# A retention and FFN sandwich: the output projection by seven products of halves, and a reordered first FFN round

## The chip, the cores and the metric

The kernel runs on one core of a Trainium2 chip. The metric is the device time of one execution in microseconds (us), as the median of several runs. A profile is one further execution, taken by the hardware profiler. The engines are named as in the profile: PE is TensorE (matmuls), PEld its weight loads, DVE is VectorE, ACT is ScalarE, POOL is GpSimd, and SP is the engine whose queue issues nearly all DMA transfers.

## The reference

The input x holds 4 sequences of 1024 tokens with 512 features, all float32. Two residual branches follow each other: a gated retention layer and a gated FFN.

```python
def _L0_attn_ref(x, Wq, Wv, Wo, Wg, ln_gamma, ln_beta, beta):
    lam = _decay_lambda(beta)
    q = (x @ Wq.T).reshape(Bsz, Ls, NHEAD, HEAD_DIM)
    v = (x @ Wv.T).reshape(Bsz, Ls, NHEAD, HEAD_DIM)
    ret = _retention_scan(v, lam)          # state = lam * state + v, along the tokens
    out = (q * ret).reshape(Bsz, Ls, D)
    out = _layernorm(out, ln_gamma, ln_beta)
    g = jax.nn.silu(x @ Wg.T)
    out = out * g
    return out @ Wo.T

def _L0_ffn_ref(x, gate_w, up_w, down_w, gate_scale, up_scale, down_scale):
    gate = jax.nn.silu(_quantized_matmul(x, gate_w, gate_scale))   # 512 -> 1536
    up = _quantized_matmul(x, up_w, up_scale)                      # 512 -> 1536
    fuse = gate * up
    return _quantized_matmul(fuse, down_w, down_scale)             # 1536 -> 512, weights rounded to fp8

x = x + _layernorm(_L0_attn_ref(_layernorm(x), ...))
x = x + _layernorm(_L0_ffn_ref(_layernorm(x), ...))
```

## The kernel before

The 4096 tokens are cut into eight blocks of 512 (`NB`), and a block into four token tiles of 128 (`NS`). A block passes through a retention part (class `Retention`) and an FFN part (class `Ffn`). The main loop, lines 985 to 1200, runs over blocks `t` and, within one, over twelve steps `i`, one for each 128 of the 1536 hidden features. I call the twelve steps of one `t` a round. In round `t` the FFN of block `t` (`f`, fed by `a`) is computed, and between its matmuls the retention part of block `t+1` (`b`), the end of the FFN of block `t-1` (`l`), and the loads and the first norm of block `t+2` (`n`) are interleaved. The order is written out by hand: every call goes through `InOrder` (line 66), which keeps each engine's instructions in program order. So an instruction that waits holds back everything behind it on its engine, and a DMA that waits holds back the later ones of SP.

In each step TensorE does a group `pfg` (gate), a group `pfu` (up) and, two steps late, a group `pd` (down). Each is eight matmuls with 512 moving columns, for which the normalized input and the fused product are split in two parts of reduced precision: an upper part, cast by ScalarE (`upper_of`, the cast in `fuse`), and a remainder, subtracted on VectorE (`rest_of`, `rest`). The groups `pfg` and `pfu` write into the two PSUM buffers `pf`. ScalarE applies Silu to `pfg` (into a `gate` tile, tag `sg`, three buffers), and VectorE multiplies with `pfu`.

The projections q, v and g of blocks 0 and 1 are plain float32 matmuls. From block 2 on (`FAST = 2`), `product` computes them in the Winograd form of Strassen's scheme: features and tokens are halved, and seven products of halves, each of eight passes of 256 columns, take the place of eight. Sums of the weight halves are made once (`weight_sums`) and kept in DRAM (`keep_sums`); sums of the input halves are made on POOL for each block (`input_sums`, into `t_sums`). The operands are fetched through a ring of four tiles (`w_ring`): after each product the fetch for the fourth product ahead is issued on SP (`fetch_weights`). Partial results are added on ScalarE and VectorE in `mids`.

The output projection `o` (line 657) is a plain float32 group for each token tile, called in steps 7 to 10. Then, for each token tile: `o_moments` (mean and variance of the PSUM tile on VectorE, the power -1/2 on POOL), `x1_of` (norm, from block 2 on with `center_scale` on VectorE; residual addition on POOL; the store `kept` on SP), `x1_moments`, `x1n_of` (norm), and the turn to features on partitions. Tiles 0 to 2 are turned by VectorE and DMA (`move_x1n`, `turn_by_blocks`: a 32x32 transpose, four stores `mxs` to DRAM, one load), tile 3 by TensorE (`turn_x1n`, rows `pt`). `upper_of` and `rest_of` then fill `x1nT`, which the first `pfg` of the next round reads.

Meanwhile `norm_x` and `send_x` make and store the normalized tiles of `n` in steps 6 to 9; from block 3 on the tile and its transposed copy lie in a single buffer:

```python
self.pair = work.tile([P, 2, D], F32, tag="xn", name=f"xn_{self.t}_{s}", bufs=1)
```

`fetch_x` loads them back turned (`xnT`). Two more threads run in rounds 0 and 1. `rounds` and `units` round the FFN weights in pieces on VectorE and ScalarE in round 0. `find_over` reads the rounded weights on ScalarE in round 1 (24 passes, rows `seen`; the list `look` says how many in which step). The mean and the variance over features for block `b` are matmuls with a constant matrix, rows `mu` and `var`; their input is split by `halves`, called in step 3 before `mean` and in step 4 before `var`.

## Time and profile before

| quantity | value |
|---|---|
| median of 3 runs | 984.01 us (983.93 to 984.02) |
| the profiled execution | 983.95 us |
| its span, first to last instruction | 982.1 us |
| granted TensorE clock | 0.998 |
| matmuls `po` (8 passes for each of 32 token tiles) | 256 records, 114.5 us busy |
| matmuls `pt` (turns on TensorE) | 44 records, 6.8 us busy |
| products of blocks 2 to 7 | 21 for each block |
| rounds 2 to 5, one round | 117.5 us |

The page of the profile gives busy times of each engine, the chain of waits that ended last, and groups of like instructions. All kernel instructions are recorded under line 74, since `InOrder` issues them; so groups are told apart by tile names (`po<-wo_sb,y` is written to `po`, reading `wo_sb` and `y`). In a timeline, a row has the start, the duration, the engine and the operation; `x8` is a run of eight, and a bracket at its end tells how long the engine stood idle before it and who ended that wait. Matmuls are pipelined and the ends of their records are modelled, so that the distance between starts is the surer measure.

### The profile page before, as it was taken

To read this page: it belongs to the slowest core of one execution; us is meant where nothing else is said; L and a number is where in the kernel's file an instruction comes from. 1 tells how busy PE (TensorE), PEld (TensorE's weight loads), DVE (VectorE), ACT (ScalarE), POOL (GpSimd) and SP (SyncE) were. 2 spreads that over 40 slices of the span, in tenths; PEclk is the share of its full clock that TensorE was granted. 3 is DMA by queue.
4 is the path that set the end of the run, shared out by engine and by line. 5 is a ranking of instruction groups with operands and counts; after the bars stand their busy time and mean duration, and the time that the engine had idled before them with its cause. 6 is when DMAs were issued, how large, how long until landed. Compare 5 with 4: busy or idle time off the path is not lost.

```text
span 982.1 us, 11265 instructions
## 1 busy us (share of the span) xinstructions
PE 963.9 (98%) x3950; PEld 734.3 (75%) x3950; DVE 663.3 (68%) x1019; ACT 369.9 (38%) x556; POOL 266.7 (27%) x346
## 2 busy tenths in 40 slices
PE   9999999989999999999999999999999999999996
PEld 7456656678876888678876788768887788877885
DVE  5996979655667667675686666766667765756445
ACT  3546655467645125221432215321152211512223
POOL 1405121412324033240513305133141322322020
PEclk9999999999999999999999999999999999999999
DMA  9311413752416426253243623245241542213021
GB/s 300 119 65 65 130 63 94 228 161 75 151 53 156 128 82 225 80 143 120 86 129 93 176 77 116 87 131 151 83 150 59 135 140 76 75 37 113 1 86 43
DMA packets 90936, 110.07 MB, mean 112 GB/s; under 512 B 8064, under 2 KB 55424, under 8 KB 90880
## 3 DMA queue, kind: packets, MB, share of 16 engines
q1 hardware_dynamic: 90016, 108.70, 36.5%
q8 instruction: 31, 0.51, 0.2%
q10 hardware_dynamic: 864, 0.66, 0.2%
q14 instruction: 25, 0.20, 0.1%
HBM read 76.56 MB, written 32.77 MB: 111 GB/s over the span
## 4 chain that ended last, share of the span: by engine, by line
PE 84%; DVE 7%; ACT 4%; POOL 2%; DMA 1%; issue 1%; SPq 0%; DVEq 0%; POOLq 0%; ACTq 0%
PE pfu L74 15%; PE pfg L74 15%; PE pd L74 15%; PE pq L74 10%; PE pv L74 10%; PE po L74 9%; PE pg L74 9%; DVE scr L74 1%; DVE st L74 1%; DVE gate L74 1%; PE idle L74 1%; DVE xs L74 1%; DVE fuse L74 1%; DMA xnT<-mx 1%; POOL sqsum L74 1%
## 5 line engine op out<-in xcount | busy, mean ns | idle before, releaser
L74 PE MATMUL pfu<-x1nT,up_sb 128*128 128x512 f32 x768 | 211.5, 417 | 0.3 <-DVE gate L74 0.3
L74 PE MATMUL pfg<-x1nT,gate_sb 128*128 128x512 f32 x768 | 195.4, 396 | 1.4 <-ACT gate L74 1.4
L74 PE MATMUL pd<-down_sb,fuse 128*128 128x512 f32 x720 | 186.5, 400 | 0.0
L74 PEld LDWEIGHTS pfu<-x1nT,up_sb 128*128 128x128 f32 x768 | 144.4, 188 | 43.0 <-issue 13.4
L74 PEld LDWEIGHTS pfg<-x1nT,gate_sb 128*128 128x128 f32 x768 | 144.2, 188 | 31.7 <-ACT gate L74 1.8
L74 PEld LDWEIGHTS pd<-down_sb,fuse 128*128 128x128 f32 x720 | 134.9, 188 | 27.4
L74 ACT CAST fuse<-gate 128x512 fp32r<-128x512 f32 x90 | 55.7, 618 | 235.5 <-DVE gate L74 235.5
L74 ACT ACTIVATE gate<-pfg,gs_sb 128x512 f32<-128x512 f32 x96 | 65.7, 685 | 193.0 <-PE pfg L74 192.9
L74 DVE SCALAR_TENSOR_TENSOR gate<-pfu,us_sb,gate 128x512 f32<-128x512 f32 x96 | 71.7, 747 | 72.3 <-PE pfu L74 69.8
L74 PE MATMUL po<-wo_sb,y 128*128 128x512 f32 x256 | 114.5, 592 | 0.0
L74 POOL TENSOR_SCALAR mv<-mv 128x1 f32<-128x1 f32 (+1 forms) x82 | 19.9, 243 | 299.0 <-DVE mv L74 298.0
L74 PEld LDWEIGHTS po<-wo_sb,y 128*128 128x128 f32 x256 | 48.2, 189 | 50.3 <-issue 46.3
L74 DVE TENSOR_TENSOR fuse<-gate,fuse 128x512 fp32r<-128x512 f32 x90 | 74.5, 827 | 12.1 <-ACT fuse L74 12.1
L74 POOL TENSOR_TENSOR ysum<-y 128x256 f32<-128x256 f32 (+1 forms) x14 | 14.0, 1000 | 189.9 <-DVE y L74 189.9
L74 POOL TENSOR_TENSOR x<-x,x1n 128x512 f32<-128x512 f32 x32 | 46.8, 1463 | 45.6 <-DVE x1n L74 36.7
L74 DVE BATCH_NORM_STATS2 st<-x 128x6 f32<-128x512 f32 x64 | 43.6, 681 | 13.7 <-POOL x L74 11.3
L74 POOL TENSOR_TENSOR mv<-mv,nhalf 128x1 f32<-128x1 f32 (+1 forms) x75 | 46.3, 617 | 6.2
L74 PE MATMUL pg<-t_sums,w_ring 128*128 128x256 f32 x192 | 45.6, 380 | 0.6 <-ACT mids L74 0.6
L74 PE MATMUL pv<-t_sums,w_ring 128*128 128x256 f32 x192 | 45.4, 379 | 0.8 <-POOL t_sums L74 0.8
L74 PE MATMUL pq<-t_sums,w_ring 128*128 128x256 f32 x192 | 45.3, 379 | 0.0
L74 PEld LDWEIGHTS pg<-t_sums,w_ring 128*128 128x128 f32 x192 | 35.9, 189 | 7.3 <-ACT mids L74 2.0
L74 PEld LDWEIGHTS pv<-t_sums,w_ring 128*128 128x128 f32 x192 | 36.2, 189 | 6.6 <-POOL t_sums L74 1.0
(150 smaller groups left out, 1337.3 us busy)
## 6 DMA issues: line engine op xcount, KB each, us to landing
kept<-x SPq DMA_DIRECT2D x32, 256.0 KB, 2.1
x<-kept SPq DMA_DIRECT2D x32, 256.0 KB, 4.1
x<-in_x SPq DMA_DIRECT2D x28, 256.0 KB, 4.1
out<-d SPq DMA_DIRECT2D x27, 256.0 KB, 2.0
xnT<-mx SPq DMA_DIRECT2D x24, 256.0 KB, 4.9
w_ring<-dsum_v SPq DMA_DIRECT2D x24, 256.0 KB, 2.7
w_ring<-dsum_q SPq DMA_DIRECT2D x24, 256.0 KB, 2.6
w_ring<-dsum_g SPq DMA_DIRECT2D x24, 256.0 KB, 2.7
```

The source lines that it names most:

```text
L74: return lambda *args, **kwargs: tc.keep_in_program_order(op(*args, **kwargs))
```

## The change

The output projection of blocks 2 to 7 becomes a fourth family of products, "o": seven products with halves of y as stationary operand (`left`) and halves or sums of the output weights from the ring as moving operand. `output_sums` makes four weight sums in place in round 1, step 0, and `keep_sums("o")` stores them. `y_sums` makes two sums of y on VectorE (step 6) and two on POOL (step 7). `add_o` copies two products on ScalarE and adds five on VectorE; the results lie in `mids` and take the place of the PSUM tiles `po`. The products stand three in step 7, three in step 8, one in step 9. What follows is regrouped by pairs of token tiles: `x1_of` for these blocks goes to ScalarE (`shift_scale`), tile 2 is turned on TensorE as well as tile 3, and the loads of tiles 0 and 1 are issued after all eight of their stores. For `n`, the norms of tiles 1 and 2 fall in step 7, tile 3 and `fetch_x` in step 8. In step 11 the fused product comes ahead of the norm of tile 3, the remainder of step 10 comes after both, and the v products are taken in the order 1, 2, 6.

In round 0, `halves` is called at the end of steps 2 and 3, with the weight rounding of step 3 moved behind the mean and partly behind the second call; the gate tile g of chunk 0 for block 1 takes a buffer of tag `tok` instead of `sg`; in steps 10 and 11 the stores of the g sums come after the stores of tile 2's turn, the norm of tile 3 goes to VectorE, and a product stands ahead of its turn. In round 1 the passes of `find_over` are distributed otherwise.

```diff
-        sp.dma_start(dst, m)
+        return lambda: sp.dma_start(dst, m)
...
-    order = [("v", j) for j in (1, 6, 2, 7, 4, 5, 3)]
+    order = [("v", j) for j in (1, 2, 6, 7, 4, 5, 3)]
     order += [("q", j) for j in (1, 6, 2, 7, 4, 5, 3)]
     order += [("g", j) for j in (1, 2, 6, 7, 4, 5, 3)]
-    banks = {"v": {1: 0, 6: 1, 5: 0}, "q": {1: 1, 6: 0, 5: 1}, "g": {1: 0, 6: 0, 5: 1}}
+    order += [("o", j) for j in (1, 2, 6, 5, 3, 7, 4)]
+    banks = {
+        "v": {1: 0, 6: 1, 5: 0}, "q": {1: 1, 6: 0, 5: 1},
+        "g": {1: 0, 6: 0, 5: 1}, "o": {1: 0, 6: 1, 5: 0},
+    }
...
+    def output_sums():
+
+        v = woT.rearrange("(c p) f -> p c f", p=P)
+        b11, b12, b21, b22 = (wo_sb[:, i : i + 2, o : o + H] for i in (0, 2) for o in (0, H))
+        operands["o"] = {1: v[:, 0:2, 0:H], 2: v[:, 2:4, 0:H], 3: v[:, 2:4, H:D]}
+        made["o"] = {5: b11, 7: b12, 6: b22, 4: b21}
+        dve.tensor_tensor(b11, b12, b11, ALU.subtract)
+        dve.tensor_tensor(b12, b22, b12, ALU.subtract)
+        dve.tensor_tensor(b22, b22, b11, ALU.subtract)
+        dve.tensor_tensor(b21, b21, b22, ALU.subtract)
...
+                    if k == "o":
+                        left, right = self.left[j][:, c, ts(o, P)], w[:, c, :]
+                    else:
+                        left, right = w[:, c, ts(o, P)], self.right[j][:, c]
...
+            if k == "o":
+                return self.add_o(j, bank)
             c12, p1, s167 = (mids[:, m] for m in (1, 2, 3))
+            if k == "v" and self.t == FAST:
+
+                if j == 1:
+                    self.p1 = work.tile([P, 2, H], F32, tag="rstd", name="p1", bufs=1)
+                p1 = self.p1
...
+        def y_sums(self, *which):
+            y = self.y
+            a11, a12, a21, a22 = (y[:, c : c + 2, ts(h, H)] for h in range(2) for c in (0, 2))
+            s1, s2, s3, s4 = (t_sums[:, k] for k in range(4))
+            self.left = {1: a11, 2: a12, 3: s4, 4: a22, 5: s1, 6: s2, 7: s3}
+            ops = {
+                1: (dve, s1, a21, a22, ALU.add), 2: (dve, s2, s1, a11, ALU.subtract),
+                3: (pool, s3, a11, a21, ALU.subtract), 4: (pool, s4, a12, s2, ALU.subtract),
+            }
+            for k in which:
+                engine, dst, x, y, op = ops[k]
+                engine.tensor_tensor(dst, x, y, op)
...
+        def add_o(self, j, bank):
+
+            by_tile = mids.rearrange("p (r s) h f -> p r s h f", r=2)
+            c11, c12, c21, c22 = (by_tile[:, r, :, h, :] for r in range(2) for h in range(2))
+            if j == 1:
+                act.copy(c21, bank)
+            elif j == 2:
+                act.copy(c11, bank)
+            elif j == 6:
+                dve.tensor_tensor(c12, bank, c21, ALU.add)
...
+            if j in (3, 4):
+                for s in (0, 1) if j == 3 else (2, 3):
+                    self.po[s] = mids[:, s].rearrange("p h f -> p (h f)")
...
             home = big if self.t == 0 and c == 3 else work
-            tag = "fuse" if home is big else "sg"
-            self.g[c] = home.tile([P, TB], F32, tag=tag, name=f"g_{self.t}_{c}", bufs=3)
+            tag, bufs = ("fuse", 3) if home is big else ("tok", 4) if self.t == 1 and c == 0 else ("sg", 3)
+            self.g[c] = home.tile([P, TB], F32, tag=tag, name=f"g_{self.t}_{c}", bufs=bufs)
...
         def x1_of(self, s):
             self.x1n[s] = work.tile([P, D], F32, tag="tok", name=f"x1n_{self.t}_{s}", bufs=4)
-            self.center(self.x1n[s], self.po.pop(s), self.mvo[s])
+            center = shift_scale if self.fast else self.center
+            center(self.x1n[s], self.po.pop(s), self.mvo[s])
...
+        def x1n_of(self, s, center=None):
+            (center or self.center)(self.x1n[s], self.xt[s], self.mvo.pop(s))
...
+    look = [(2, 3), (2, 3), (2, 3), (1, 0), (0, 0), (0, 2)]
+    look += [(0, 1), (0, 1), (1, 0), (1, 1), (0, 0), (1, 0)]
...
-            if t > 0 and (t > 1 or i):
+            if t > 0 and (t > 1 or i) and not (fast and i == 11):
...
-                if i == 10:
-                    keep_sums("g")
...
-            if fast and i in (0, 1, 2, 3, 4, 5, 6):
+            if fast and i < 10:
                 b.product()
...
             if b and not fast and i == 3:
-                b.halves()
-                units()
-                rounds(3, now=False)
                 units()
                 b.g_of(0)
                 b.mean()
                 b.center_y()
+                n.stats(2)
                 n.stats(3)
                 n.rstd()
                 n.shift()
             if b and not fast and i == 4:
-                b.halves()
                 rounds(3, now=False)
...
-            if b and 7 <= i <= 10:
+            if b and not fast and 7 <= i <= 10:
                 b.o(i - 7)
             if b and i == 8:
                 b.new_x1nT()
-            if b and i >= 8:
+            if b and not fast and 8 <= i < 11:
                 b.x1n_of(i - 8)
-            if b and 8 <= i < 11:
-                b.move_x1n(i - 8)
-            if b and i >= 9:
+            if b and not fast and 8 <= i < 11:
+                load = b.move_x1n(i - 8)
+                if i == 10:
+                    keep_sums("g")
+                load()
+            if b and not fast and 9 <= i < 11:
                 b.upper_of(i - 9)
-            if b and 7 <= i <= 10:
+            if b and not fast and 7 <= i <= 10:
                 b.o_moments(i - 7)
-            if n and i == 11:
-                n.input_sums(1, 2, 3, 4)
+            if fast and i == 7:
+                b.y_sums(3, 4)
+            if fast and i == 9:
+                b.x1_moments(0)
+                b.x1_moments(1)
+            if fast and i == 10:
+                b.x1_of(2)
+                b.x1_of(3)
             units()
             f.up(i)
+            if n and i == 11:
+                n.input_sums()
+                n.product()
             f.fuse(i)
+            if b and i == 11:
+                b.x1n_of(3, center_scale)
+            if fast and i == 11:
+                f.rest(10)
+            if n and i == 11:
+                n.input_sums(*((3, 4) if fast else (1, 2, 3, 4)))
+            if t == 0 and i == 11:
+                b.upper_of(2)
+            if fast and i == 9:
+                loads = []
+                for s in range(2):
+                    b.x1n_of(s)
+                    loads.append(b.move_x1n(s))
+                for load in loads:
+                    load()
+                if n:
+                    n.input_sums(1, 2)
+            if fast and i == 11:
+                for s in range(2):
+                    b.upper_of(s)
+                    b.rest_of(s)
             if t == 0 and i == 4:
                 b.rstd_y()
-            if n and i == 11:
-                n.product()
-                if t:
-                    b.turn_x1n(3, "pf")
-                    b.upper_of(3)
+            if n and t and i == 11:
+                b.turn_x1n(2, "pf")
+                b.upper_of(2)
             if t == 2 and i == 0:
                 next(passing)
             if fast and i < 6:
             if fast and i == 6:
                 b.gate_y(0)
                 b.gate_y(1)
+                b.y_sums(1, 2)
+            if n and t > 0 and i == 8:
+                n.norm_x(3, True)
+                n.send_x(3)
+            if fast and i in (7, 8):
+                b.product()
+            if n and t > 0 and i == 8:
+                n.fetch_x()
+            if fast and i == 8:
+                b.o_moments(0)
+                b.o_moments(1)
+                b.x1_of(0)
+                b.x1_of(1)
+            if fast and i == 9:
+                b.o_moments(2)
+                b.o_moments(3)
+            if fast and i == 10:
+                b.x1_moments(2)
+                b.x1_moments(3)
+                b.x1n_of(2)
             if t == 0:
-                if i < 8 and i != 3:
+                if i == 3:
+                    rounds(2, now=False)
+                    b.halves()
+                    units()
+                    rounds(1, now=False)
+                elif i < 8:
                     rounds(3, now=False)
+                if i == 2:
+                    b.halves()
                 f.rest(i)
-                if i < 3:
+                if i < 2:
                     n.stats(i)
-            for _ in range((look[i] + 1) // 2 if t == 1 else 0):
-                next(search)
 
             if l and not b and i in (4, 5):
                 l.stats(2 * i - 8)
                     l.rstd()
             if n and i == 6:
                 n.new_xnT()
-            if b and 7 <= i <= 10:
+            if b and not fast and 7 <= i <= 10:
                 b.x1_of(i - 7)
-            if b and i >= 9:
+            if b and not fast and i >= 9:
                 b.rest_of(i - 9)
-            if n and t > 0 and 6 <= i <= 9:
-                n.norm_x(i - 6, True)
-                n.send_x(i - 6)
+            if n and t > 0 and i in (6, 7):
+                for s in ([0], [1, 2])[i - 6]:
+                    n.norm_x(s, True)
+                    n.send_x(s)
+            for _ in range(look[i][1] if t == 1 else 0):
+                next(search)
             if t == 0 and i in (5, 6):
                 n.send_x(2 * i - 10)
                 n.send_x(2 * i - 9)
-            if n and i == (9 if t else 7):
+            if n and t == 0 and i == 7:
                 n.fetch_x()
             if b and n and i == 11 and t:
-                b.rest_of(3)
+                b.rest_of(2)
             if t == 0 and i in (8, 9):
                 keep_sums("vq"[i - 8])
 
             elif l and i < 2 and (b or i == 0):
                 l.down(NI - 2 + i if b else NI - 1)
             if b and not n and i == 11:
+                b.turn_x1n(2)
+                b.upper_of(2)
+                b.rest_of(2)
                 b.turn_x1n(3)
                 b.upper_of(3)
                 b.rest_of(3)
                 f.down(NI - 2)
 
-            if t == 0 and i == 11:
+            if n and i == 11:
+                if t == 0:
+                    n.product()
                 b.turn_x1n(3, "pf")
                 b.upper_of(3)
                 b.rest_of(3)
-            if fast and i < 3:
+            if fast and (i < 3 or i in (7, 8)):
                 b.product()
             if fast and i == 2:
                 l.stats(2)
                 b.var()
                 b.rstd_y()
             if n and i == 11:
-                n.products(2)
+                n.products(2 if t else 1)
             if n and t > 0 and i == 5:
                 n.stats(0)
                 n.stats(1)
+            if t == 1 and i == 0:
+                output_sums()
+                keep_sums("o")
             if t == 0 and i == 9:
                 w_ring = wpool.tile([P, RING, 2, H], F32, tag="wv_sb", name="w_ring")
             if t == 0 and i in (9, 10):
```

## The prediction

> **What bounds the kernel now.** I read the page first: busy shares, then the chain of waits.
>
> ```profile
> PE 963.9 (98%) x3950; PEld 734.3 (75%) x3950; DVE 663.3 (68%) x1019; ACT 369.9 (38%) x556; POOL 266.7 (27%) x346
> PE 84%; DVE 7%; ACT 4%; POOL 2%; DMA 1%; issue 1%; SPq 0%; DVEq 0%; POOLq 0%; ACTq 0%
> ```
>
> TensorE is the bound. A busy share hides where it waits, so next the windows of one FFN round each:
>
> ```profile
> 100.00:206.00 106.00, 100.16 (x372) 68.87 (x371) 84.05 (x117) 56.45 (x86) 28.20 (x33) 1.00 0.43 133
> 322.00:440.00 118.00, 117.91 (x501) 93.31 (x500) 79.91 (x127) 36.10 (x56) 34.79 (x45) 1.00 0.44 132
> 440.00:557.00 117.00, 116.91 (x495) 92.44 (x494) 79.40 (x123) 33.76 (x52) 34.80 (x45) 1.00 0.39 114
> ```
>
> Columns: length, then PE, PEld, DVE, ACT, POOL busy. The first row (round 0, old path) lacks 6 us; later rounds lack 0.1, so there only fewer matmuls or new waits can matter. The timeline of PE at step 11 of a later round gives the prices:
>
> ```profile
> 546.08 1.98 PE L74 MATMUL pfg<-x1nT,gate_sb 128*128 128x512 f32 x8
> 547.90 1.98 PE L74 MATMUL pfu<-x1nT,up_sb 128*128 128x512 f32 x8
> 549.71 1.89 PE L74 MATMUL pv<-xnT,w_ring 128*128 128x256 f32 x8
> 551.69 0.63 PE L74 MATMUL pt<-ident,x1n 128*128 128x128 f32 x4
> 552.08 2.09 PE L74 MATMUL pd<-down_sb,fuse 128*128 128x512 f32 x8
> 554.00 1.89 PE L74 MATMUL pv<-t_sums,w_ring 128*128 128x256 f32 x8
> 555.73 1.89 PE L74 MATMUL pv<-xnT,w_ring 128*128 128x256 f32 x8
> ```
>
> Read starts, since ends overlap: a gate, up or down group costs 1.82 us, a product 1.73 (554.00 to 555.73). The same timeline has the waits of PE, all in rounds 0 and 1:
>
> ```profile
> 118.43 0.50 PE L74 MATMUL mu<-half,mean_r 128*128 128x512 f32 x1 [0.49 <-DVE half L74]
> ...
> 128.43 0.50 PE L74 MATMUL var<-half,mean_r 128*128 128x512 f32 x1 [0.58 <-ACT half L74]
> ...
> 143.60 2.14 PE L74 MATMUL pfg<-x1nT,gate_sb 128*128 128x512 f32 x8 [1.41 <-ACT gate L74]
> ...
> 196.84 0.66 PE L74 MATMUL pt<-ident,x1n 128*128 128x128 f32 x4 [0.65 <-ACT x1n L74]
> 198.25 1.99 PE L74 MATMUL pv<-t_sums,w_ring 128*128 128x256 f32 x8 [0.75 <-POOL t_sums L74]
> 201.66 1.96 PE L74 MATMUL pv<-xnT,w_ring 128*128 128x256 f32 x8 [1.42 <-ACT x1nT L74]
> ...
> 252.96 1.99 PE L74 MATMUL pg<-t_sums,w_ring 128*128 128x256 f32 x8 [0.64 <-ACT mids L74]
> ```
>
> **What the Trainium skill says.** "SBUF — State Buffer", section "Who interferes with whom": VectorE with two SBUF inputs, or in a 2-port mode, and GpSimd exclude each other for whole instructions. The trace agrees: a fuse remainder that takes 0.66 took 1.78 at 546.52, until POOL's addition ended.
>
> ```profile
> 546.09 1.67 POOL L74 TENSOR_TENSOR x<-x,x1n 128x512 f32<-128x512 f32 x1 [1.61 <-DVE x1n L74]
> 546.52 1.78 DVE L74 TENSOR_TENSOR fuse<-gate,fuse 128x512 fp32r<-128x512 f32 x1
> 550.07 1.47 DVE L74 TENSOR_SCALAR x1n<-x,mv 128x512 f32<-128x512 f32 x1 [0.95 <-POOL mv L74]
> ```
>
> "TensorE: Matmul & The Clock Gate", "Back-to-back issue gap", has the isolated gap follow the free size (N/2.4 + 2.5 ns). In the trace half the width costs half: 3.44 us for eight passes of 512, 1.73 for eight of 256, so halving the tile isn't taxed.
>
> **The change, part by part.**
>
> Output projection of blocks 2 to 7. Removed: four groups po, each 3.44 (four steps of 8.89 less three groups of 1.82): 13.76. Added: seven products of 1.73: 12.11. So -1.65 a block. Also added: token tile 2 is turned on TensorE, not by DMA. At 904.15 a turn with no wait put 0.35 before one group and 0.12 on it: +0.45. Net -1.2 a block, -7.2 in six. The DMA turn it saves costs PE nothing today.
>
> New waits of these steps. I count from the start of step 7's gate group (510.52 in round 3), other durations from rows.
> - Product 1 needs y of chunk 1. VectorE finished it at 512.75, +2.23. Its first two passes last 0.43, not the 0.86 of po's, so it asks earlier: 0.2 a block.
> - VectorE then makes two sums (0.69 each) and POOL two (1.3 to 1.45), which shut VectorE out: the step 7 gate product ends near +7.6 instead of +6.4. Behind it on ScalarE: the fuse cast, the copy of products 1+2 (0.59), then two xn (0.81 each). Blocks from 3 on hold xn and its turned copy in one single-buffered pair, so the second xn waits for the first's store: turned at +10.4, landed 2.3 later, +12.8; xn 13.6, turn 14.3, addition of product 6 15.0, remainder 15.7, addition of product 5 16.4. Product 3 accumulates in product 5's bank and stands at +16.0. Wait 0 to 0.8; I take 0.3.
> - Moments, ScalarE's x1, POOL's addition, second moments and x1n of tile 2 end near +38.5; its turn stands at +39.3. Tile 3's x1n, once shut out by POOL's input sums (1.3), ends at +40.7; turn +41.7. Then four remainders of 0.68 behind step 10's end at +45.4, one group of the next round needs them at +45.8, and product 6's addition ends +47.6 where product 7 stands at +47.5. Slack 0.4 with two exclusions counted; bounds 0 and 1.6, I take 0.4.
> Sum 0.9 a block, 5.4 in six: this part nets -1.8. In round 6 no next block's products stand between the last turn and the next gate group, only one down group of 1.82; VectorE has less there too, and I keep the same 0.9.
>
> Moved on SP, in order of issue: the stores of xn go out in steps 6 to 8 and the four loads of xnT in step 8, ahead of both kept stores; the two tiles' eight mxs stores follow the x1n of step 9 (near +29.5 and +31), their loads come after all eight, at about +33.3 and +35.6, and land 2.7 to 3.7 later, by +39.3. ScalarE wants them after the fuse cast, at +40.7: covered by 1.4; if that cover goes, the next round's first gate group waits one for one. xnT, asked for at +22, lands by +28 (5.8 at most from the trace's chain) and is wanted by POOL at +28.4 and by PE at +37.6.
>
> Cost nothing: the eight more weight loads' traffic (2.6 to 3.1 us landing against four products of ring), since fetches are issued four products ahead; POOL's two sums, behind 27% load; ScalarE's x1 passes (0.20+0.29+0.78 for each of four tiles, 5.1 a block, which frees VectorE of four of 0.80), 38% load. If the queue of SP blocked (kept waits for POOL's addition), the ring still covers over 10 us. Four sums of wo in round 1 (0.69 each) and their stores lie in VectorE's gaps; without these, up to 2.8. The search keeps its 24 passes, moved.
>
> Round 0, steps 3 to 6. mu started its group 1.03 late (117.15 to 118.77 is 1.62; 482.59 to 483.18, unhindered, 0.59); halves now stand before that step's rounding. var: 1.56 late (next group due at 127.94, came at 129.50); its halves stand before one rounding. Step 6's gate group: 1.56 (143.60 against 142.04): ScalarE's Silu waited for a buffer that g of chunk 0 held; that tile moves to the tok buffers. Bounds 0 and 4.15. VectorE is late next: reciprocal (3.35) and rounding stay, 84 of 106 us are busy. I take 3.6.
>
> Round 0, step 11: waits with pipeline loss 1.0, 0.95 and 1.7. x1n of tile 3 goes from ScalarE to VectorE, a product comes before the turn, tile 2's move is sent before the four stores of wg sums (mxs started at 191.41, after stores that began at 188.70; its landing ended the last wait). Next: POOL's second sum at about 198.2 and remainder 3. Bounds 0 and 3.65; I take 3.1. Step 11's 0.32 for DVE gate stays.
>
> Round 1: ScalarE's copy for the second product of g is freed of one search pass (1.56+0.19) ahead of it: 0.8 goes. xn is fetched a step earlier: the 0.29 at 314.61 goes, 0.4 with loss. Together 1.2.
>
> Sum: -1.8 -3.6 -3.1 -1.2 = -9.7. The profiled execution took 983.95 (span 982.1 and 1.85 around it), 0.06 under the median 984.01: 974.3.
>
> **Rivals.**
> A, nothing waits: -7.2 -4.15 -3.65 -1.2 = -16.2: 967.8. For it: ScalarE and POOL are idle most of each round. Against: VectorE at 68% with late due times.
> B, block 0's gains hold but the new products lose about 0.5 a block: -7.9 +3 = -4.9: 979.1. That is waits of 1.7 a block, between my 0.9 and the 2.6 of the upper bounds (0.2, 0.8, 1.6). For it: each stands within a microsecond of its due time. Against: they are not independent; a late product 3 gives VectorE the same time back later.
> C, slower: POOL shuts VectorE out at step 11. Besides the two exclusions counted, both remainders from x1n (1.62 at worst for 0.68: +1.9) and POOL's own additions (1.73 for 1.30: +0.8) lie ahead of the next round's gate group; less slack 0.4 that is 2.3, with the other 0.9 3.2 a block, 19.2 in six, against gains of 7.2+3.6+3.1+1.2 = 15.1: +4.1, 988.1. It decides from 2.5 a block. For it: exclusion shown at 546.52 and 550.07. Against: only the few at step 11 hit in before.
> D, no change: the same waits at 2.5: 984.
>
> **How the numbers follow.** Forecast (971 to 977) 0.50, A 0.18, B 0.16, D 0.04, C 0.12. Range: A's middle part below and half of C above are left out: 968.5 to 984.5. Faster by over 0.2% (2 us, about what a measurement tells) 0.84, within 0.04, slower 0.12.
>
> **What would show it.** PE's row po: 336 records of 256 columns for six blocks beside 64 of 512; pt 68 records, not 44. mu, var and the step 6 gate group without a wait in round 0. A round of 117.5 should become 117.2. po waiting for DVE mids at step 8, and pfg or pv for DVE x1nT or mids at the next round's start, are the waits I price. Wrong would be: PE idle of over 2 us a round there, or round 0 still losing over 3 us.

## The result, and the profile after

The changed kernel takes 974.39 us (median of four runs, 973.13 to 975.49) against 984.01 before: ratio 0.9898, 95% interval 0.9881 to 0.9916. The prediction was 974.3. The total agrees to 0.1 us. That closeness is luck: the four runs lie 2.4 us apart, and two terms of the prediction's sum were off by about 2 us each, in opposite directions.

The page of the changed kernel, busy shares and chain of waits:

```profile
PE 957.6 (98%) x4118; PEld 765.0 (79%) x4118; DVE 678.8 (70%) x1036; ACT 406.4 (42%) x637; POOL 284.9 (29%) x358
PE 85%; DVE 6%; DMA 3%; ACT 2%; POOL 2%; issue 1%; SPq 0%; DVEq 0%; POOLq 0%; ACTq 0%
```

TensorE is as full as before, with 6.3 us less work. DVE, ACT and POOL took up 15.5, 36.5 and 18.2 us more. The windows of one FFN round each (columns as in the prediction):

```profile
100.00:206.00 106.00, 103.22 (x392) 72.94 (x391) 90.30 (x121) 59.32 (x88) 29.50 (x33) 1.00 0.49 146
322.00:440.00 118.00, 118.00 (x534) 99.24 (x533) 81.75 (x130) 42.19 (x70) 37.28 (x47) 1.00 0.48 147
440.00:557.00 117.00, 116.80 (x527) 98.02 (x526) 80.58 (x126) 40.04 (x66) 37.75 (x47) 1.00 0.44 127
```

Round 0, the first row, lost 5.8 us of TensorE and now loses 2.8, just under the 3 that the prediction named as a sign of being wrong. VectorE is busy 90 of its 106 us. The waits of PE (total, times, longest), without three that belong to the start, ahead of round 0, and are in the kernel before as well:

```profile
...
PE pv L74 <- DMA w_ring<-dsum_v: 1.1, 1, 1.1
PE pt L74 <- DVE x1n L74: 1.1, 1, 1.1
...
PE pfu L74 <- DVE gate L74: 1.0, 1, 1.0
PE pfg L74 <- ACT gate L74: 0.7, 1, 0.7
PE pfg L74 <- DVE x1nT L74: 0.6, 1, 0.6
...
PE po L74 <- issue: 0.2, 1, 0.2
```

The `mu` and `var` waits are gone. New are `w_ring`, `x1nT` and a larger `pfu` wait at round 0's step 11, `pfg` in round 1, `pt` in round 5, `po` in round 3.

To see where the time went I cut both profiled executions at TensorE's first `mu` matmul, which stands once in every FFN round (at step 3), and at step 6's gate group in round 0. The profiled execution of the changed kernel took 975.49, the longest of its four.

| stretch | before | after | difference | predicted |
|---|---|---|---|---|
| start to `mu` of round 0 | 117.15 | 118.04 | +0.89 | 0 |
| to step 6's gate, round 0 | 26.45 | 22.80 | -3.65 | -3.6 |
| to `mu` of round 1 | 102.57 | 101.75 | -0.82 | -3.1 |
| to the end | 735.93 | 731.11 | -4.82 | -1.8 - 1.2 = -3.0 |
| span | 982.1 | 973.7 | -8.4 | -9.7 |

I don't put the first row down to the change: the first row of warm-up matmuls took 6.33 us here and 5.29 in the profile of before, and in the profiles below, all of the changed kernel or of edits of it, the stretch is 117.5 to 118.4. With one profile of before, a small share of the change in it isn't excluded. Such shifts, and chance waits of about a microsecond, are why single spans are compared by stretches here.

The last row by rounds, `mu` to `mu`, rounds 1 to 5 and the rest: before 118.91, 117.51, 117.55, 117.52, 117.56 and 146.88; after 117.95, 116.27, 116.74, 116.64, 117.72 and 145.79. The differences are -0.96, -1.24, -0.81, -0.88, +0.16 and -1.09. The undisturbed round after is round 2, 116.27, 1.24 under 117.51. The net is that of the prediction, but its parts aren't. From step 7's gate group to step 11's, rounds 2 to 5 took 35.57 before, and round 2 takes 34.13 now: 1.44 less, not 1.65. Some 0.15 of the rest is product 1: in rounds 1 to 5 it takes longer than the other products up to the start of the next group, 1.68 against 1.53 here in round 3:

```profile
506.55 2.03 PE L74 MATMUL po<-w_ring,y 128*128 128x256 f32 x8
508.23 2.21 PE L74 MATMUL pfu<-x1nT,up_sb 128*128 128x512 f32 x8
510.28 1.89 PE L74 MATMUL po<-w_ring,y 128*128 128x256 f32 x8
511.81 2.20 PE L74 MATMUL pd<-down_sb,fuse 128*128 128x512 f32 x8
```

From step 11's gate group to the next `mu` the round grew by 0.2, not by 0.45. The turn before had itself stood 0.25 late: in the prediction's lines 549.71 to 551.69 is 1.98, where a product takes 1.73, and x1n ended at 551.54. That wait is too short for the list, and it is gone now. The operation counts, from the view of the tiles `po` and `pt`:

```profile
L74 PE MATMUL po<-w_ring,t_sums x192: 377/379/454, 279.6 to 876.9; 128*128 128x256 f32 x192
L74 PE MATMUL po<-w_ring,y x144: 377/379/483, 272.4 to 880.5; 128*128 128x256 f32 x144
L74 PE MATMUL po<-wo_sb,y x64: 590/592/592, 70.7 to 181.2; 128*128 128x512 f32 x64
```

336 narrow records beside 64 wide ones, and 68 of `pt`, as foreseen. And step 11 of round 3, PE's timeline:

```profile
542.96 1.89 PE L74 MATMUL pv<-xnT,w_ring 128*128 128x256 f32 x8
544.68 0.60 PE L74 MATMUL pt<-ident,x1n 128*128 128x128 f32 x4
545.04 2.10 PE L74 MATMUL pd<-down_sb,fuse 128*128 128x512 f32 x8
546.98 0.60 PE L74 MATMUL pt<-ident,x1n 128*128 128x128 f32 x4
547.41 1.89 PE L74 MATMUL pv<-xnT,w_ring 128*128 128x256 f32 x8
549.14 1.89 PE L74 MATMUL pv<-t_sums,w_ring 128*128 128x256 f32 x8
550.68 2.20 PE L74 MATMUL pfg<-x1nT,gate_sb 128*128 128x512 f32 x8
```

The two turns and the down group between them fill 544.68 to 547.41, 2.73, which is 0.91 more than a group of 1.82: 0.45 for a turn. No idle time stands here in rounds 2 and 3.

### The profile page after: what moved, and what is told of

It reads as the page before. It is cut to its first block, busy times and chain, and to the rows that moved or that the text cites. A ratio compares the mean times of both kernels' runs of the same rounds, so it can differ in the third digit from the quotient of the medians.

```text
span 973.7 us, 11796 instructions
## 1 busy us (share of the span) xinstructions
PE 957.6 (98%) x4118; PEld 765.0 (79%) x4118; DVE 678.8 (70%) x1036; ACT 406.4 (42%) x637; POOL 284.9 (29%) x358
## 4 chain that ended last, share of the span: by engine, by line
PE 85%; DVE 6%; DMA 3%; ACT 2%; POOL 2%; issue 1%; SPq 0%; DVEq 0%; POOLq 0%; ACTq 0%
PE pfg L74 15%; PE pfu L74 15%; PE pd L74 14%; PE pq L74 10%; PE pv L74 10%; PE pg L74 9%; PE po L74 8%; DMA xnT<-mx 1%; DVE scr L74 1%; DVE st L74 1%; DVE y L74 1%; PE pt L74 1%; ACT x1n L74 1%; PE idle L74 1%; DVE gate L74 1%
## 5 line engine op out<-in xcount | busy, mean ns | idle before, releaser
L74 PE MATMUL pfu<-x1nT,up_sb 128*128 128x512 f32 x768 | 205.2, 409 | 1.0 <-DVE gate L74 1.0
L74 PE MATMUL pfg<-x1nT,gate_sb 128*128 128x512 f32 x768 | 198.3, 400 | 1.3 <-ACT gate L74 0.7
L74 PE MATMUL pd<-down_sb,fuse 128*128 128x512 f32 x720 | 188.9, 404 | 0.0
L74 DVE SCALAR_TENSOR_TENSOR gate<-pfu,us_sb,gate 128x512 f32<-128x512 f32 x96 | 71.7, 747 | 58.9 <-PE pfu L74 56.2
L74 POOL TENSOR_SCALAR mv<-mv 128x1 f32<-128x1 f32 (+1 forms) x82 | 23.1, 282 | 263.4 <-DVE mv L74 260.2
L74 DVE TENSOR_TENSOR fuse<-gate,fuse 128x512 fp32r<-128x512 f32 x90 | 78.7, 874 | 6.2 <-ACT fuse L74 6.2
L74 POOL TENSOR_TENSOR x<-x,x1n 128x512 f32<-128x512 f32 x32 | 41.6, 1301 | 15.7 <-ACT x1n L74 15.4
L74 PE MATMUL po<-w_ring,t_sums 128*128 128x256 f32 x192 | 45.4, 379 | 0.2 <-issue 0.2
L74 PEld LDWEIGHTS po<-w_ring,t_sums 128*128 128x128 f32 x192 | 36.2, 189 | 6.2 <-issue 0.6
```

The lines of the kernel that those rows point to most:

```text
L74: return lambda *args, **kwargs: tc.keep_in_program_order(op(*args, **kwargs))
```

## Experiments

Each is an edit of the changed kernel. Times are medians. The experiments ran in three sets, each on a chip of its own and beside the kernel before, which took 984.5 to 984.7; the changed kernel, run again in the last set, took 974.81. The runs of one version lie up to 4 us apart, so small differences are read from stretches of the trace and not from medians.

### Round 0, undone as a whole and in three parts

The three parts: `halves_back` puts the two halves, the rounding calls and tile 2's statistics where they were:

```diff
-                if i == 3:
-                    rounds(2, now=False)
-                    b.halves()
-                    units()
-                    rounds(1, now=False)
-                elif i < 8:
+                if i < 8 and i != 3:
                     rounds(3, now=False)
-                if i == 2:
-                    b.halves()
...
             if b and not fast and i == 3:
+                b.halves()
                 units()
+                rounds(3, now=False)
+                units()
                 b.g_of(0)
...
             if b and not fast and i == 4:
+                b.halves()
                 rounds(3, now=False)
```

`g0_back` gives block 1's g of chunk 0 its old buffer:

```diff
-            tag, bufs = ("fuse", 3) if home is big else ("tok", 4) if self.t == 1 and c == 0 else ("sg", 3)
+            tag, bufs = ("fuse", 3) if home is big else ("sg", 3)
```

`step11_back` restores round 0's step 11: products 1, 6, 2 in that order, POOL's four sums ahead of the up group, x1n of tile 3 on ScalarE, the stores of wg's sums at the start of step 10, the turn ahead of the second product:

```diff
...
+            if t == 0 and i == 11:
+                n.input_sums(1, 2, 3, 4)
             units()
             f.up(i)
-            if n and i == 11:
+            if n and t and i == 11:
                 n.input_sums()
                 n.product()
             f.fuse(i)
+            if t == 0 and i == 11:
+                n.product()
...
```

`block0_back` is all three together.

> Only the halves of y's sum and of its squares (steps 3 and 4 again instead of 2 and 3), the rounding calls and tile 2's statistics stand where they stood in the kernel before. Prediction's terms: mu 1.03 and var 1.56 late again, 2.6 of waits, of which 3.6/4.15 taken: +2.2, 976.6, with mu and var waiting and step 6's gate group not. Rival, the waits share a cause (an earlier delay gives VectorE and ScalarE time, so the later ones shrink): below +1.2, 975.6.

> Only g of block 1's chunk 0 is back in an sg buffer. Theory: ScalarE's Silu of step 6's gate waits for a buffer again and the step 6 gate group comes 1.56 later: +1.35 to +1.6, 975.9. Rival: with mu and var earlier the buffer is free in time and nothing happens: 974.4.

> Only step 11 of round 0 is in its old order: block 2's first v products 1, 6, 2 with POOL's four sums ahead of the up group, x1n of tile 3 on ScalarE, the stores of wg's sums at the start of step 10, products 6 and 2 behind the turn. Prediction's term: +3.1, 977.5. Theory of the traces (the new waits of 1.02, 1.15 and 0.61 took back most of what was gained): +1.3, 975.7. Rival: the old order without the old start of step 3 to 6 is no slower: 974.4.

> All edits of round 0 are undone in the changed kernel; the output projection by seven products and the rounds from 1 on keep their new form. Theory of the prediction's terms: round 0 was worth 3.6 (steps 3 to 6) + 3.1 (step 11) = 6.7, so 974.4 + 6.7 = 981.1. Theory of the traces (pfg of step 6 came 3.65 earlier relative to the start, step 11 only about 1.3): +5.0, 979.4. Rival: round 0's gain depends on the rest and the fast blocks gave most of the 9.6: +2.5 or less, 977 or less.

Measured, with the same cuts of the trace:

| kernel | median | `mu` to step 6's gate | to `mu` of round 1 |
|---|---|---|---|
| before | 984.01 | 26.45 | 102.57 |
| changed | 974.39 | 22.80 | 101.75 |
| halves_back | 975.72 | 24.86 | 100.67 |
| g0_back | 976.22 | 25.46 | 101.22 |
| step11_back | 975.81 | 22.81 | 102.72 |
| block0_back | 979.34 (ratio 0.9943, 0.9922 to 0.9964) | 26.44 | 102.15 |

block0_back comes out at the theory of the traces (979.4), not at the prediction's terms (981.1). Round 0 is worth 4.0 by the two stretches and 4.5 to 5.0 by the medians (against 974.81 and 974.39), not 6.7, and the rest of the gain, about 5, is in the later rounds. There block0_back takes 730.8 from `mu` of round 1 to the end, like the changed kernel's 731.1.

Over both stretches the three parts cost 0.98, 2.13 and 0.98, and the whole 4.04. Within the stretches they don't add up, and two things come out of that. First, the waits of steps 3 to 6 are not independent. With the halves put back, step 6's gate stands without a wait and 2.06 are lost there; with only the buffer put back, 2.66, where before it had cost 1.56. PE's timeline of g0_back:

```profile
143.88 2.14 PE L74 MATMUL pfg<-x1nT,gate_sb 128*128 128x512 f32 x8 [2.50 <-ACT gate L74]
```

The wait was 1.41 before. Counted from `mu`, TensorE was ready for this group 2.1 sooner than before, and the buffer came free only 1.0 sooner, so TensorE waited longer.

Second, what is lost in steps 3 to 6 is partly won back at step 11: halves_back needs 1.08 less than the changed kernel from step 6's gate on. It is the same effect from the other side: at step 11 other engines set the pace, and TensorE's head start ends as a wait. PE's timeline of the changed kernel there:

```profile
188.27 2.11 PE L74 MATMUL pfu<-x1nT,up_sb 128*128 128x512 f32 x8 [1.02 <-DVE gate L74]
...
197.24 1.97 PE L74 MATMUL pv<-t_sums,w_ring 128*128 128x256 f32 x8 [1.15 <-DMA w_ring<-dsum_v]
198.85 0.58 PE L74 MATMUL pfg<-x1nT,gate_sb 128*128 128x512 f32 x1
200.05 1.89 PE L74 MATMUL pfg<-x1nT,gate_sb 128*128 128x512 f32 x7 [0.61 <-DVE x1nT L74]
```

VectorE in the same stretch, and SP's queue:

```profile
183.06 2.84 DVE L74 TENSOR_TENSOR wg_sb<-wg_sb 128x512 f32<-128x512 f32 x4
...
193.41 1.48 DVE L74 TENSOR_SCALAR x1n<-x,mv 128x512 f32<-128x512 f32 x1 [0.30 <-POOL mv L74]
194.82 1.75 DVE L74 TENSOR_TENSOR fuse<-gate,fuse 128x512 fp32r<-128x512 f32 x1
196.50 1.74 DVE L74 TENSOR_TENSOR x1nT<-x1n,x1nT 128x512 fp32r<-128x512 f32 x1
198.16 1.25 DVE L74 TENSOR_TENSOR_SCAN y<-lam,pv 128x256 f32<-128x256 f32 x2
199.34 0.66 DVE L74 TENSOR_TENSOR x1nT<-pt,x1nT 128x512 fp32r<-128x512 f32 x1
```

```profile
188.81 2.55 SPq L74 DMA_DIRECT2D dsum_g<-wg_sb  x4
191.53 0.49 SPq L74 DMA_DIRECT2D x1n<-mxs  x1
192.07 0.65 SPq L74 DMA_DIRECT2D kept<-x  x1
192.77 1.04 SPq L74 DMA_DIRECT2D w_ring<-dsum_v  x2
```

The four sums of wg (2.84) stand ahead of step 10's gate product, so `pfu` waits. The weights of products 6 and 7 are issued behind four stores and two more transfers, and land late. They are not the only late operand: in the second profile of the same kernel, after_again, the same product waits 1.60 for POOL's `t_sums`, and no wait for `w_ring` or `x1nT` is listed. POOL's four sums make x1n, fuse and x1nT take 1.48, 1.75 and 1.74, where undisturbed rows show 0.55, 0.67 and 0.68. From x1n on VectorE stands in no listed wait until the last remainder (`x1nT<-pt`), which the next round's first gate group needs, ends at 200.00.

### Late stores and one search pass moved (early)

```diff
                 load = b.move_x1n(i - 8)
-                if i == 10:
-                    keep_sums("g")
                 load()
...
             if t == 0 and i == 10:
+                keep_sums("g")
                 t_sums = wpool.tile([P, 4, 2, H], F32, tag="wq_sb", name="t_sums")
...
-    look = [(2, 3), (2, 3), (2, 3), (1, 0), (0, 0), (0, 2)]
-    look += [(0, 1), (0, 1), (1, 0), (1, 1), (0, 0), (1, 0)]
+    look = [(2, 3), (2, 3), (2, 3), (1, 0), (0, 1), (0, 2)]
+    look += [(0, 1), (0, 1), (1, 0), (1, 0), (0, 0), (1, 0)]
```

(The buffers of the passes change at pass 19, not 18, to suit.)

> Two moves in the changed kernel. Round 0: the four stores of wg's sums are issued after the ring's fetches for products 6 and 7 at the end of step 10, not ahead of tile 2's load in step 10. Round 1: one search pass goes from step 9 to step 4. Theory: the waits for dsum_v (1.15) and for x1nT (0.61, partly by the same late queue) in round 0 and the 0.68 wait of round 1's step 11 go: -1.2 to -2.4, 972 to 973.2. Rival for round 0: POOL's second sum stands right behind, so product 6 waits for t_sums instead, as it did for 1.63 when the halves were put back: round 0 gains 0.3 or less, and the whole -0.7, 973.7.

972.83 (971.34 to 973.68). Round 1 goes from 117.95 to 116.52: its ScalarE search pass had waited for a DMA with step 10's Silu behind it, and the 0.68 wait with all that followed is gone. Round 0 gained nothing: 22.80 and 101.76. The `w_ring` wait fell from 1.15 to 0.57, and `x1nT`'s rose from 0.61 to 1.18. The rival was right in kind, though another wait than the one it named stood behind. The last remainder on VectorE ends 59.2 after step 6's gate group in early, as it does in the changed kernel.

### An eighth product

```diff
+            if k == "o" and j == 4:
+                for o in range(2):
+                    for c in range(2):
+                        pe.matmul(
+                            bank[:, o], self.left[j][:, c, ts(o, P)], w[:, c, :],
+                            start=False, stop=True, skip_group_check=True,
+                        )
             fetch_weights()
```

> The last product of the output projection (4, in step 9) is multiplied twice in each of the six fast blocks, so these blocks' o is not that of the reference; nothing else differs. It prices a product where it stands. Theory, TensorE is the bound there and nothing else was near: +1.73 a block, +10.4, 984.8, as slow as the kernel before, so that seven against eight products is the whole of the part's gain. Rival, the chain of o behind it (additions, moments, x1) sets step 11: the delay adds waits for pt and x1nT of up to 1 a block: +12 to +16, 986 to 990. Other rival, waits of 0.9 a block absorb a part: +5 to +8, 980 to 982.

983.64 (ratio 0.999, 0.9981 to 0.9998): +9.25 in medians. By stretches the rounds 1 to 5 and the rest grew by 1.74, 1.70, 1.64, 1.37, 0.30 and 1.74. Where nothing waits, a product costs what its matmuls take. Where the changed kernel waits (rounds 4 and 5), the longer product only fills the wait; it is 8.5 in all beside the first profile of the changed kernel and 9.1 beside the second. So seven products instead of eight is the part's gain, and the chain behind it adds nothing when o comes 1.7 later.

### Tile 2 turned by DMA again (dma2)

```diff
                 b.x1_moments(3)
                 b.x1n_of(2)
+                b.move_x1n(2)()
...
             if n and t and i == 11:
-                b.turn_x1n(2, "pf")
                 b.upper_of(2)
...
             if b and not n and i == 11:
-                b.turn_x1n(2)
                 b.upper_of(2)
```

> Token tile 2 of the fast blocks is turned by DMA again (VectorE's 32-blocks, four stores, one load at the end of step 10), not on TensorE in step 11. Theory of the prediction's price: -0.45 a block, -2.7 in six, 971.7, if the load lands by step 11's copy. Rival: x1n of tile 2 is made only at the end of step 10, so the landing comes some 5 us later, behind the due time of the upper copy, and the next round's first gate group waits about 1 to 3 a block: +3 to +15, 977 to 989.

993.65 (990.4 to 994.46), above the rival's range. The turn of 0.45 bought a lot: without it six gate groups now wait 9.7 us together for ScalarE's copy, which waits for the load, and 1.7 for the remainders. The last of these waits, 3.49 for the copy, shows something more. PE's timeline of dma2 at the start of round 7, then windows from there:

```profile
909.47 4.20 PE L74 MATMUL pfg<-x1nT,gate_sb 128*128 128x512 f32 x8 [3.49 <-ACT x1nT L74]
913.47 3.03 PE L74 MATMUL pfu<-x1nT,up_sb 128*128 128x512 f32 x8
916.34 2.00 PE L74 MATMUL pd<-down_sb,fuse 128*128 128x512 f32 x8
```

```profile
909.00:911.00 2.00, 1.48 (x3) 0.88 (x4) 1.86 (x3) 0.42 (x1) 0.00 (x0) 0.50 0.80 277
...
913.00:915.00 2.00, 2.00 (x6) 1.57 (x5) 0.00 (x0) 0.69 (x1) 0.00 (x0) 0.50 0.00 0
915.00:917.00 2.00, 2.00 (x8) 1.57 (x8) 0.40 (x1) 0.00 (x0) 0.00 (x0) 0.83 0.00 0
```

Around the end of the idle 3.49 us the granted clock (third column from the right) falls to 0.50, and it stays there until about 915.7, where 0.83 is the mean of its window: some 6.7 us. The two groups behind it take 6.87 (909.47 to 916.34), where the same two take 3.79 in the changed kernel (897.93 to 901.72): 3.1 us more. This wait cost nearly twice its length.

### Two causes in the fast blocks (fast_waits)

```diff
                 for load in loads:
                     load()
-                if n:
-                    n.input_sums(1, 2)
...
                 b.x1_moments(3)
+                if n:
+                    n.input_sums(1, 2)
                 b.x1n_of(2)
...
-            if self.t < 3:
+            if self.t != 3:
                 sq = work.tile([P, D], F32, tag="ret", name=f"xs_{self.t}_{s}")
```

> Two causes are taken away in the fast blocks: POOL's first two input sums stand behind the moments of tiles 2 and 3 in step 10 (not in step 9, where they waited for xnT and POOL's powers behind them), and the turned copy of xn lies in a buffer of its own, so the second xn of step 7 no longer waits for the first one's store. Theory: the 1.11 wait of pt in round 5 and the 0.2 to 0.36 at product 3 in round 3 go: -0.7 to -1.5, 973.3. Rival, these were chance delays of single transfers, and other waits of that size come: within 0.5 of 974.4. For the prediction's 0.3 a block at product 3 to be right the gain in six blocks would have to be 1.8 from the buffer alone.

978.75, ratio 0.9942 (0.9927 to 0.9956): slower than the changed kernel by 4.4, which neither theory had. (Block 3 keeps the single buffer here; blocks 4 to 7 have the new one.) Rounds 2 to 5 take 117.0 to 117.2. The 1.1 of round 5 is gone, and each of these rounds loses 0.7 to 1.0 against 116.27, around the next round's first gate group. Round 1 takes 120.09, 2.1 more than in the changed kernel, with a wait of 1.48 for `x1nT` before that group. VectorE in fast_waits at step 11 of round 3:

```profile
547.64 1.78 DVE L74 TENSOR_TENSOR fuse<-gate,fuse 128x512 fp32r<-128x512 f32 x1
549.34 3.43 DVE L74 TENSOR_TENSOR x1nT<-x1n,x1nT 128x512 fp32r<-128x512 f32 x2
552.70 1.27 DVE L74 TENSOR_TENSOR x1nT<-pt,x1nT 128x512 fp32r<-128x512 f32 x2
```

POOL now adds four sums at 546.17 to 552.23, not two, and the two remainders from x1n take 3.43 instead of 1.28. The last remainder ends at 553.97, behind the due time of the gate group. The move of POOL's sums is the cause and not the buffer, since best2 below has the buffer too and loses nothing. This is rival C of the prediction, made to happen: C needed both x1n remainders shut out, and here they are. In the changed kernel POOL's sums end just before, and the last remainder ends 0.66 ahead of the gate group (550.02 against 550.68 in round 3).

### Versions that go further

`best1` is early, with the sums of wg behind step 10's gate product, and block 2's input sums 3 and 4 on VectorE behind the last remainder. `best2` adds the separate buffer of fast_waits for the turned xn (not its move of POOL's sums) and makes tile 3's xn right behind step 8's gate group:

```diff
-            if n and t > 0 and i == 8:
-                n.norm_x(3, True)
-                n.send_x(3)
             if fast and i in (7, 8):
...
+            if n and t > 0 and i == 8:
+                n.norm_x(3, True)
+                n.send_x(3)
             units()
             f.up(i)
```

> The changed kernel as it is, beside the versions of this call on the same chip: 974.4 within 1.2, with waits in round 0's step 11 of some 2.8, 0.7 in round 1 and 1.1 in round 5.

> The version with the late stores of wg's sums and the moved search pass (972.8), and two moves more in round 0: the four sums of wg stand behind step 10's gate product on VectorE, and block 2's input sums 3 and 4 are made by VectorE behind the last x1nT remainder, not by POOL. Theory, VectorE was held by the wg sums (pfu's 1.02) and shut out by POOL's sums 3 and 4 (x1n 1.49, fuse 1.75, x1nT 1.75; pfg's 1.18): both waits go, -1.0 to -2.2, 971.2. Rival, the w_ring fetch or the chain of x1n of tile 3 stands right behind: -0.5 or less, 972.4.

> best1 and, in the fast blocks, tile 3's xn made right behind step 8's gate group (not behind its fuse product), with the turned copy of xn in a buffer of its own. Theory: the load of xnT starts some 2 us earlier, POOL's sums of step 9 no longer wait for it in round 5, and the 1.0 to 1.1 of pt there goes: another -1.1, 970.1. Rival: ScalarE's xn stands ahead of the fuse cast and VectorE's turn ahead of the gate product, which delays the additions of o by as much, so product 3 or 7 waits up to 0.5 a block: +0 to +3, 971 to 974.

after_again 974.81, best1 972.99 (ratio to before 0.9874, 0.9857 to 0.9892), best2 971.56 (0.9863, 0.9848 to 0.9878). best2 is the fastest of all that ran, 3.2 under the changed kernel. best1 gains nothing on early. Its `pfu` wait fell from 1.02 to 0.22 and its `x1nT` wait from 1.18 to 0.68, but x1n of tile 3 comes later (`pt` waits 0.55, `t_sums` 0.46): VectorE has the same work before it either way, and the stretch from step 6's gate to `mu` of round 1 is 101.73, against 101.74 in after_again. best2's step does what its theory said. All its rounds from 2 to 5 take 116.24 to 116.30, and round 1 116.47. Which of its two further edits takes away round 5's wait (1.26 in best1) isn't separated.

## Why the prediction was right, and where it was not

**The bound.** Right: TensorE alone sets the rounds from 1 on. The eighth product shows it, 1.70 for 1.73 in an undisturbed round.

**The price of the products and turns, -1.2 a block.** Right in the sum: 1.24 in round 2, and 116.24 to 116.30 against 117.51 to 117.56 in best2, where no listed wait is left in these rounds. The parts were off in opposite directions. The products give 1.44 and not 1.65; 0.15 of that is product 1's wait, which the prediction booked apart. The turns cost 0.2 and not 0.45, since the wait of 0.25 ahead of the old turn went; the prediction shows the lines of that wait, but counted only 0.1 us of idle time in a later round.

**The new waits, 0.9 a block or 5.4 in six.** This is the first mis-sized term. With the 1.2 that round 1 was to gain, 4.2 were to be given back in these rounds; the trace gives back 6 times 1.24 less 4.82, 2.6, of which 1.45 lie in round 5 alone, from a wait that had not been booked. The schedule behind the term was close. Product 3 in round 3, first ScalarE, then VectorE, then PE:

```profile
517.90 0.81 ACT L74 ACTIVATE xn<-x,mv 128x512 f32<-128x512 f32 x1 [2.87 <-DMA mx<-xn]
```

```profile
520.55 0.68 DVE L74 TENSOR_TENSOR mids<-po,mids 128x512 f32<-128x512 f32 x1
```

```profile
521.33 1.97 PE L74 MATMUL po<-w_ring,t_sums 128*128 128x256 f32 x8 [0.20 <-issue]
```

Counted from step 7's gate group at 504.74, the addition ends at +16.5 (predicted 16.4), and the product starts 0.36 late. The single-buffered pair holds ScalarE up as the prediction said. But 0.36 happened once in six blocks, and not at all in after_again, where 0.3 had been booked for each. Product 1's 0.2 was right: in rounds 1 to 5 it waits about 0.15 (1.68 against 1.53), too short for the list, and that is already in the 1.24. At step 11's end both exclusions happened as counted, and a slack of 0.66 (0.4 predicted) was left, so the 0.4 booked for the wait was not needed. The step that failed was to take a point inside each interval of bounds as its mean, in the terms 0.3 and 0.4: where the best estimate of the schedule has slack, the wait is mostly nothing.

**xnT "lands by +28".** Wrong in round 5, the largest of the new waits. POOL there in the changed kernel, then ScalarE:

```profile
769.33 1.29 POOL L74 TENSOR_TENSOR t_sums<-xnT 128x512 f32<-128x512 f32 x1 [2.45 <-DMA xnT<-mx]
```

```profile
773.26 0.29 ACT L74 ACTIVATE nb<-nb,mv 128x1 f32<-128x1 f32 x1 [3.40 <-POOL mv L74]
```

Step 7's gate group stood near 738.1 (`mu` of round 5 and 27.9), so xnT came at about +31. POOL waited in order, its powers for tiles 2 and 3 behind the sums, then x1 on ScalarE, then x1n, then the turn: 1.1. best2 removes exactly this. The last store of xn landed late in that one round (4.4 us against 2.2 in round 4). In the seven profiles of this order in which it took 3.7 us or more the wait came, at 0.9 to 1.3; in the three in which it took 2.1 to 2.4 (step11_back, eighth, dma2) it did not. Why the store is late stays open. In best2 xnT is asked for 5 us earlier (46.6 after `mu`, against 51.7).

**Round 0, steps 3 to 6, -3.6.** Right in size: -3.65. PE's timeline after:

```profile
118.04 1.03 PE L74 MATMUL mu<-half,mean_r 128*128 128x512 f32 x2
118.91 2.01 PE L74 MATMUL pfu<-x1nT,up_sb 128*128 128x512 f32 x8
...
127.42 1.03 PE L74 MATMUL var<-half,mean_r 128*128 128x512 f32 x2
128.29 2.01 PE L74 MATMUL pfu<-x1nT,up_sb 128*128 128x512 f32 x8
...
140.84 1.98 PE L74 MATMUL pfg<-x1nT,gate_sb 128*128 128x512 f32 x8
```

The way to it was luck in part. `mu` and `var` without a wait take 0.87 each here (118.04 to 118.91), while the prediction subtracted 0.59, read in a later round. So their waits were 0.75 and 1.3, not 1.03 and 1.56, and with step 6's 1.56 the whole loss was 3.6, not 4.15. All of it went. The prediction had taken off 0.55 for a late VectorE, which did not show. Neither part would have come alone as priced: the buffer by itself keeps 1.6 (halves_back, 24.86 against 26.45), but the halves by themselves keep only 1.0 (g0_back, 25.46).

**Round 0, step 11, -3.1.** The second mis-sized term: 0.82 by the trace beside before, and 0.97 by undoing it alone (102.72 against 101.75; the medians, 975.81 and 974.39, are 1.4 apart, but the runs overlap). The three old waits did go or shrink. What failed is "Step 11's 0.32 for DVE gate stays", and that nothing was said of the weights of product 6. The gain of 3.65 just before brings TensorE to step 11 earlier, and the engines there don't come earlier with it: 0.32 became 1.02. It is 1.01 in step11_back too, and 0.33 in g0_back, where TensorE comes later. "Next: POOL's second sum at about 198.2 and remainder 3" was right about what ends the step, not about its size: in after_again product 6 waits 1.60 for POOL's sum, and in both profiles VectorE's last remainder ends 59.1 to 59.2 after step 6's gate group.

**Round 1, -1.2.** Both old waits went, and a new one of 0.68 came from a search pass that waited for a DMA; with what followed it cost 1.4 (117.95 against 116.52 in early). It was not foreseen: the prediction called the search "moved" and asked nothing of its buffers' releasers.

**The rivals.** A (nothing waits) is what best2 nearly reaches in the rounds, not in round 0. B had the two parts the wrong way round. C's mechanism is real, as fast_waits shows, at 0.7 to 1.0 a round in rounds 2 to 5 and not 3.2; a slack of 0.66 us kept it away in the changed kernel. D (984) is excluded by the interval.

Two slips in the working changed little. Seven products add seven fetches a block to the ring, not "eight more weight loads". And the exclusion hit not only at step 11 before: a fuse remainder 3.2 us after `mu` took 1.51 in each of rounds 2 to 6.

## What to carry to other kernels

A wait before the bounding engine is a difference of two times, and only one of them moves when that engine is made faster: after each gain, work out all later waits again with the new arrival, above all in a stage where another engine is nearly full. Book a wait only where the schedule puts the supplier behind the due time; where it has slack, book nothing and keep the wait for the range. Before an engine's slack is spent on moved work, look at which engine it shuts out at that moment, since two more additions of POOL at step 11 cost 0.7 to 1.0 a round here.

## What the runs showed of the hardware

With an idle TensorE of 3.49 us the granted clock fell to 0.50 for some 6.7 us (dma2), and 3.1 us were lost beside the wait. The Trainium skill, "TensorE: Matmul & The Clock Gate", "Part 1: The HAM clock gate", says that the clock falls to half after an idle window of about 3.4 us and comes back after as long a busy one. The fall agrees with this. The return took longer than one such time here: about 6.2 us from the first matmul behind the wait (909.47 to 915.7). The wait of 2.50 in g0_back didn't do it: the next group started 1.97 after the one behind the wait, where it was 1.98 after the wait of 1.41 before, and 1.82 where nothing waited in the changed kernel.

Three different orders of round 0's step 11 (the changed kernel in two profiles, early, best1) need 101.73 to 101.76 from step 6's gate to round 1's `mu`, though the waits in them lie at quite different places. What they share is VectorE's last remainder, which ends 58.9 to 59.2 after that gate group in all four profiles. A wait that is named there says little about what its removal gives.
